# A cross-attention kernel whose whole program stands in another order, with the banks of its scores and the shares of VectorE and GpSimd dealt out anew

## The chip, the cores and the metric

The kernel runs on one core of a Trainium2 chip. A core has five engines, each with an instruction stream of its own that it works off in order: TensorE (PE in the profile; PEld is its weight load), VectorE (DVE), ScalarE (ACT), GpSimd (POOL) and SyncE (SP, which here issues nearly all DMAs). They wait for one another through semaphores. TensorE writes to PSUM, which this kernel uses as eight banks of 128 x 512 float32; the other data lie in SBUF. The metric is the device time of one execution in microseconds, as the median of several runs.

## The reference: cross-attention with two key sets

For two batches of 2048 tokens with 640 channels, and 154 context tokens with 1024 channels (77 of text, 77 of "ip"), the reference computes, in float32:

```python
q = split_heads(x @ Wq.T, 20)                    # 20 heads of 32 channels
k, v = text @ Wk.T, text @ Wv.T                  # 77 keys
k_ip, v_ip = ip @ Wk_ip.T, ip @ Wv_ip.T          # 77 more keys
out = softmax(q k / sqrt(32)) v + softmax(q k_ip / sqrt(32)) v_ip
return out @ Wo.T + bo + x
```

The two softmaxes are separate: each row of 154 scores has two maxima and two sums, of 77 scores each.

## The kernel before, in words

The 20 heads are taken four at a time: a chunk `c` of 128 channels holds four heads of 32 channels, and there are five chunks. A pair (batch `b`, chunk `c`) is a number q = 5b + c from 0 to 9. The 2048 tokens of a batch are two halves of 1024. A unit u = 2q + half, from 0 to 19, is a pair and a half of the tokens; its 1024 tokens are eight tiles of 128 rows, in three blocks s = 0, 1, 2 of three, three and two tiles (`GROUPS`). So there are 60 blocks, 40 wide ones (1848 scores in each partition) and 20 narrow ones (1232).

The order of the program is not left to a planner. One string, `SCHEDULE`, holds 1064 words; the loop at its end emits one word after the other (`emit`), and each engine gets its instructions in the order in which the words that use it stand. So a word's place sets its turn on its own engine, and what it waits for follows from the tiles. The words:

- `q.u.h@n` (L194, TensorE): the queries of unit u for half h of its tokens, in bank n. `cq` (L204, ScalarE) scales them out to SBUF.
- `k.c.t@n`, `v.c.t@n` (L133, TensorE): a projection of keys or values for chunk c, text or ip. `ck` and `cv` (L688, L690, ScalarE) copy them out. `LK.n` loads a weight block for them, `LQ.q` one for queries, `LX.u.h` a block of tokens of the second batch. `SQ.c` (L143, VectorE) transposes the values in squares, `VW` writes them to memory outside the core and `VS` spreads them back.
- For each block s of unit u: `Rs.u@banks` (L226, TensorE) makes the scores of four heads at once, with 32 rows of the array for each head and one bank for each; four digits name the four banks, a single digit 0 or 1 means the lower or upper four. `K` (L238, ScalarE) copies the four banks to SBUF, `M` (L251, VectorE) takes the maxima, `S` (L265) subtracts them, `E` (L272, ScalarE) is the exponential, `D` (L297, VectorE) the sums, `I` (L304, VectorE) their reciprocals, `N` (L309) the normalisation, `T` (L316, VectorE) a transposition in squares of 32. `S` and `N` run on GpSimd, or on VectorE where the word ends in `.d`.
- `A.q@banks` (L325, TensorE): attention times values for both units of pair q, once their six blocks are transposed. `CA.q` (L348, L352, ScalarE) copies the result out.
- First batch's output: `m1` to `m7` (L483, L493) are seven products by half blocks in the manner of Strassen, for each of four groups of tokens, `G` (L424, GpSimd or VectorE) the sums of their token side, `W0` and `W1` (L394, GpSimd) those of the weights, `cm` (L508, L512, VectorE) adds a product to the sum. `o`, `p`, `z` (L464) are the products for the last 128 output channels, `co` and `yz` add them. `fe` fetches the old tokens for a sum, `st` stores a sum.
- Second batch's output, the last part: `F` (L848, TensorE) are 33 products in two halves, `V` (L826, L828) and `X` (L834) their sums of weights and tokens, on VectorE (`.d`) or GpSimd (`.p`), and `Y` (L794, L796, VectorE) adds products to the outputs, which leave as they are done.

Ahead of the schedule stands a fixed beginning: loads, the first queries (in banks 4, 5 and 6) and the first two key projections (banks 2 and 7).

What sets the order around the change is thus the string alone, plus the waits that follow from shared tiles: a bank is written again only once its last reader is done; the scores in SBUF have three zones, so that a unit's copies wait for the attention step that read the zone last; a weight slot is loaded again once its last product is done.

Of the kernel before, what the change touches and what calls it, by code (L numbers as in the profile page):

```python
# [9 lines left out]
F32 = mybir.dt.float32  # L10
# [10 lines left out]
def kernel(  # L21
# [523 lines left out]
    for t in range(2):  # L545
# [227 lines left out]
    for c, stages in enumerate(chains_of):  # L773
        for _, text in stages:
            for _, t in terms(text):
                for h in range(NH):
                    o = int(t[0]), NH * int(t[1]) + h
# [113 lines left out]
```

## Time and profile before

| | us |
|---|---|
| median of 3 runs | 497.94 (497.68 to 498.39) |
| the profiled execution | 498.71 |
| its span, first to last instruction | 496.9 |
| TensorE busy | 490.1 |
| VectorE busy | 441.1 |
| GpSimd busy | 403.7 |
| ScalarE busy | 241.8 |

How to read it: busy time is the union of an engine's instructions as the profile shows them. A matmul's end is modelled and neighbours overlap, so that TensorE can be shown busy while it waits a little. The groups by line give the count, the busy time, the mean length of one instruction in ns, and, behind a bar, the time that the engine was idle just before them with what ended that idle time. In the chain that ended last each row is a start, a length, and the work that the end of the program hung on at that time. `R0.0` and the like in the text are words of the schedule.

The second batch's last part begins behind `A.9` (427 us); ahead of it the scores of both batches, their projections and the first batch's output share TensorE.

### The profile page before, as it was taken

Reading aid. Unit: us, or ns where it says so; the run is one execution under the profiler, and the core shown is the slowest. Engines: PE = TensorE matmul, PEld = TensorE weight load, DVE = VectorE, ACT = ScalarE, POOL = GpSimd, SP = SyncE. Lnnn points to the kernel's source line nnn. Section 1 sums busy time; section 2 is a strip of 40 time slices with the busy share of each in tenths; the row PEclk is TensorE's granted clock in tenths of the full one; section 3 lists DMA queues with packets and bytes.
Section 4 is the critical chain, followed back from the end, with each engine's and each line's share of the span. In section 5 each row is a group of like instructions: output and inputs, shape, how many; then the busy total and the mean of one; then the engine's idle time right before and its main releaser. Section 6 shows DMA issues by size and latency. Waiting matters only on the chain.

```text
span 496.9 us, 9747 instructions
## 1 busy us (share of the span) xinstructions
PE 490.1 (99%) x4114; PEld 288.3 (58%) x4114; DVE 441.1 (89%) x404; ACT 241.8 (49%) x423; POOL 403.7 (81%) x173
## 2 busy tenths in 40 slices
PE   8999999999999999999999999999999999999997
PEld 5658547648647556456655655744766475444442
DVE  0078999999989989998999999799899999999886
ACT  1177557757747568567516635545764443100000
POOL 0079969999989999997995899799599999378770
PEclk9999999999999999999999999999999999999999
DMA  8990543520843835615677079345616012510026
GB/s 258 355 245 12 148 107 84 155 71 22 223 133 80 252 107 162 227 19 154 232 232 247 22 237 319 88 152 176 198 50 175 3 45 64 170 57 29 0 105 233
DMA packets 66988, 70.15 MB, mean 141 GB/s; under 512 B 3712, under 2 KB 46720, under 8 KB 66944
## 3 DMA queue, kind: packets, MB, share of 16 engines
q1 hardware_dynamic: 66224, 68.81, 44.5%
q8 instruction: 32, 0.52, 0.4%
q10 hardware_dynamic: 720, 0.72, 0.4%
q14 instruction: 12, 0.10, 0.1%
HBM read 58.21 MB, written 11.30 MB: 140 GB/s over the span
## 4 chain that ended last, share of the span: by engine, by line
PE 89%; DVE 6%; DMA 3%; SPq 1%; ACT 1%; issue 0%; DVEq 0%
PE bank L194 33%; PE bank L848 11%; PE bank L325 11%; PE bank L226 10%; PE bank L133 9%; PE bank L483 9%; PE bank L464 4%; PE bank L493 2%; DVE pb L316 2%; DMA aT<-in_L_xattn_Wk_ip_dram 2%; DMA wq<-in_L_xattn_Wq_dram 2%; DVE den L297 1%; DVE mx L251 1%; SPq L525 1%; DVE acc L508 0%; DVE acc L512 0%
## 5 line engine op out<-in xcount | busy, mean ns | idle before, releaser
L265 POOL TENSOR_TENSOR pb<-pb,mx 128x1848 f32<-128x1848 f32 (+1 forms) x55 | 162.8, 2980 | 36.0 <-DVE mx L251 35.8
L309 POOL TENSOR_TENSOR pb<-pb,rden 128x1848 f32<-128x1848 f32 (+1 forms) x59 | 172.2, 2940 | 24.0 <-DVE rden L304 21.3
L194 PE MATMUL bank<-x,wq 128*128 128x512 f32 x400 | 179.0, 599 | 0.4 <-DMA wq<-in_L_xattn_Wq_dram 0.2
L251 DVE TENSOR_REDUCE mx<-pb 128x24 f32<-128x1848 f32 (+1 forms) x60 | 109.3, 1841 | 32.2 <-ACT pb L238 32.1
L194 PEld LDWEIGHTS bank<-x,wq 128*128 128x128 f32 x400 | 74.5, 191 | 88.8 <-issue 81.2
L238 ACT COPY pb<-bank 128x462 f32<-128x462 f32 (+1 forms) x240 | 102.0, 537 | 44.5 <-PE bank L226 43.9
L272 ACT ACTIVATE pb<-pb 128x1848 f32<-128x1848 f32 (+1 forms) x60 | 94.2, 1583 | 54.7 <-POOL pb L265 53.9
L297 DVE TENSOR_REDUCE den<-pb 128x24 f32<-128x1848 f32 (+1 forms) x60 | 110.0, 1839 | 5.9 <-ACT pb L272 5.7
L316 DVE STREAM_TRANSPOSE pb<-pb 128x1920 f32<-128x1920 f32 (+1 forms) x60 | 113.9, 1923 | 0.9 <-POOL pb L309 0.8
L226 PEld LDWEIGHTS bank<-kT,qT 32*128 32x128 f32 x1280 | 45.9, 184 | 23.6 <-issue 14.2
L226 PE MATMUL bank<-kT,qT 32*128 32x154 f32 x1280 | 56.5, 305 | 1.0 <-ACT pb L238 0.7
L325 PE MATMUL bank<-pb,v 32*32 32x512 f32 x1600 | 55.2, 597 | 0.1
L204 ACT ACTIVATE qT<-bank 128x512 f32<-128x512 f32 x40 | 23.6, 597 | 52.7 <-PE bank L194 52.7
L133 PE MATMUL bank<-wo_ct,aT 128*128 128x154 f32 x320 | 45.8, 296 | 0.3 <-DMA aT<-in_L_xattn_Wk_ip_dram 0.3
L133 PEld LDWEIGHTS bank<-wo_ct,aT 128*128 128x128 f32 x320 | 43.0, 188 | 4.1 <-issue 2.7
L325 PEld LDWEIGHTS bank<-pb,v 32*32 32x32 f32 x1600 | 29.1, 103 | 23.2 <-issue 11.8
L464 PE MATMUL bank<-aT,wo_ct 128*128 128x512 f32 x80 | 36.3, 596 | 0.0
L483 PE MATMUL bank<-aT,wo_ct 128*128 128x256 f32 x128 | 32.8, 389 | 0.0
L796 DVE TENSOR_TENSOR x<-x,bank 128x512 f32<-128x512 f32 x36 | 23.6, 683 | 5.2 <-PE bank L848 4.6
L483 PEld LDWEIGHTS bank<-aT,wo_ct 128*128 128x128 f32 x128 | 23.3, 190 | 6.4 <-issue 3.7
L464 PEld LDWEIGHTS bank<-aT,wo_ct 128*128 128x128 f32 x80 | 15.0, 190 | 17.3 <-issue 17.1
L848 PE MATMUL bank<-pb 128*128 128x512 f32 x48 | 22.1, 593 | 0.0
(74 smaller groups left out, 348.0 us busy)
## 6 DMA issues: line engine op xcount, KB each, us to landing
x<-in_x_dram SPq DMA_DIRECT2D x20, 1280.0 KB, 6.9
out_dram<-acc SPq DMA_DIRECT2D x20, 256.0 KB, 2.6
x<-in_x_dram SPq DMA_DIRECT2D x18, 256.0 KB, 5.6
acc<-in_x_dram SPq DMA_DIRECT2D x16, 256.0 KB, 4.1
out_dram<-x SPq DMA_DIRECT2D x15, 256.0 KB, 2.0
v<-scr SPq DMA_DIRECT2D x40, 80.0 KB, 4.0
wq<-in_L_xattn_Wq_dram SPq DMA_DIRECT2D x9, 320.0 KB, 5.0
aT<-in_L_xattn_Wk_dram SPq DMA_DIRECT2D x5, 512.0 KB, 7.1
```

The source lines that it names most:

```text
L133: nc.tensor.matmul(keys_in(out), loaded[n][:, k, :], cT[:, k, :, t, :], start=(k == 0), stop=(k == NCC - 1))
L194: nc.tensor.matmul(pq, wqs[q % 3][:, k, :], xs[place_of(u, h)][:, k, :], start=(k == 0), stop=(k == NC - 1),)
L226: nc.tensor.matmul(ps[g][:, ts(t, 2 * L)], qTs[(u, h)][g * D : (g + 1) * D, ts(st, P)], kT[g * D : (g + 1) * D, c, b].rearrange("p t l -> ...
L238: nc.scalar.copy(keys_of(u, s)[:, :, g], ps[g][:, : n * 2 * L].rearrange("p (n l) -> p n l", n=n))
L251: nc.vector.tensor_reduce(mx, rows_of(u, s), AX.X, ALU.max, negate=by_rows(u, s))
L265: eng.tensor_tensor(rows_of(u, s), rows_of(u, s), maxs[(u, s)].unsqueeze(3).to_broadcast([P, n, 2, L]), ALU.subtract)
L272: nc.scalar.activation(e, e, AF.Exp)
L297: nc.vector.tensor_reduce(dens[(u, s)], rows_of(u, s), AX.X, ALU.add)
L309: eng.tensor_tensor(rows_of(u, s), rows_of(u, s), rdens[(u, s)].unsqueeze(3).to_broadcast([P, n, 2, L]), ALU.mult)
L316: nc.vector.transpose(p, p)
L325: nc.tensor.matmul(pa[r][g * D : (g + 1) * D, :], v4s[q % 2][rows, g, k, :], zones[rows, :, g, k, :], start=(k == 0), stop=(k == NK - 1),)
L483: nc.tensor.matmul(part, w_of[m][:, kp, op], t_of(m, b, i)[:, kp], start=(op == kp == 0 and m in (1, 2, 5)), stop=(op == 1 and kp == 1 and ...
```

## The change: the same words in another order

Every word of the one string stands in the other, once, and nothing but the string is changed. What differs:

- the order, from the first word on (before begins with block 2 of unit 0, after with block 0);
- the banks behind `@`, for nearly all score steps and for most queries, projections and products;
- the engine of some sums. Of the subtractions `S`, before has five on VectorE (S1.2, S2.9, S0.10, S2.12, S0.16), after eight (S1.0, S0.2, S1.4, S2.9, S0.10, S0.12, S1.14, S1.15). Of the normalisations `N`, before has N0.12 on VectorE, after N2.7 and N1.16. One `G` sum moves each way, nine `V` and five `X` sums each way;
- `V.P.1` moves ahead of the last transposes, and `LW`, the reload of a part of the output weights, behind the word `A.9`.

The first lines and the lines around `A.9`:

```diff
     SCHEDULE = (
-        "R2.0@2031 K2.0 M2.0 R0.0@6754 K0.0 S2.0 R1.0@1032 K1.0 M0.0 S0.0 q.1.0@7 E2.0 LK.4 M1.0 S1.0 q.1.1@2 "
-        "LK.5 D2.0 I2.0 cq.1.0 R0.1@6157 E0.0 D0.0 I0.0 cq.1.1 R1.1@0243 K0.1 M0.1 N0.0 S0.1 K1.1 k.1.0@6 M1.1 "
...
-        "p.1@4 D1.19 I1.19 D2.19 I2.19 T0.19 m4.3 fe.3.3 cm4.3 st.3.3 p.3@6 N1.19 p.2@7 T1.19 N2.19 T2.19 "
-        "X.B.d@0 A.9@0 V.H.0.d V.P.1.p V.Q.0.d V.T.0.d CA.9 V.T.1.d st.3.1 V.N.0.d X.A.d@1 V.A.0.p V.M.0.d "
...
+        "R0.0@4756 K0.0 M0.0 S0.0 LK.4 R1.0@3012 K1.0 M1.0 q.1.0@4 LK.5 R2.0@1750 K2.0 M2.0 S1.0.d q.1.1@3 "
+        "cq.1.0 LQ.3 S2.0 E0.0 D0.0 I0.0 N0.0 cq.1.1 R0.1@7651 K0.1 R1.1@0423 M0.1 K1.1 M1.1 k.1.0@7 ck.1.0 S0.1 "
...
+        "D1.19 I1.19 fe.3.3 m4.3 cm4.3 V.P.1.d st.3.3 N0.19 T0.19 N2.19 N1.19 T2.19 T1.19 p.1@4 X.L.p@3 p.0@5 "
+        "X.A.d@1 A.9@0132 CA.9 LW V.N.0.d V.G.0.p X.B.d@0 V.U.0.d V.U.1.d V.Q.0.d V.T.0.p V.E.0.d F31.1@0 "
```

Lines of after that hold the places the prediction speaks of (LK.6 and v.1.0; S1.4; N2.7; S1.15; G6.2):

```diff
+        "E1.0 E2.0 k.1.1@6 S1.1 D1.0 R2.1@0457 K2.1 T0.0 E1.1 v.0.0@1 I1.0 N1.0 LK.6 E0.1 M2.1 cv.0.0 D2.0 D1.1 "
+        "I2.0 v.0.1@7 cv.0.1 S2.1 N2.0 q.2.1@4 cq.2.1 v.1.0@5 SQ.0 ck.1.1 D0.1 I1.1 T1.0 cv.1.0 R2.2@4023 K2.2 "
...
+        "N1.3 T1.3 N2.3 q.6.0@3 cq.6.0 S0.4 E0.4 T2.3 S2.4 E2.4 M1.4 S1.4.d D0.4 I0.4 N0.4 A.1@6457 LK.12 E1.4 "
...
+        "E1.7 D2.7 I2.7 N2.7.d R2.8@2013 I0.7 N0.7 cq.9.0 R0.8@4657 D1.7 LK.19 I1.7 K2.8 M2.8 N1.7 K0.8 M0.8 "
...
+        "R2.15@3142 T1.14 m4.1 cq.16.1 E0.15 M1.15 I2.14 K2.15 R2.16@1653 q.17.0@0 fe.1.3 S1.15.d E1.15 K2.16 "
...
+        "K1.17 G6.2 G5.3 S0.17 E0.17 m6.2 cm3.2 LX.18.1 q.18.1@2 st.2.0 fe.3.0 X.I.p@2 M1.17 G4.2 T1.16 "
```

124 rows, old and new, of the table SCHEDULE are left out of this document.

## The prediction

> **What bounds the kernel now.** I read the page's busy times first, then the chain that ended last in order of time, then the busy times in five stretches, then the groups of instructions by shape, the waits, and the timeline at a few places.
>
> ```profile
> PE 490.1 (99%) x4114; PEld 288.3 (58%) x4114; DVE 441.1 (89%) x404; ACT 241.8 (49%) x423; POOL 403.7 (81%) x173
> ```
> ```profile
> 24.04 0.84 PE bank L226 x16
> 25.17 1.07 ACT pb L238 x3
> 26.29 1.07 PE bank L226 x24
> 27.35 8.78 PE bank L194 x20
> 36.13 1.78 PE bank L226 x48
> ...
> 47.48 8.58 PE bank L194 x20
> ...
> 423.53 3.49 DVE pb L316 x2
> 427.06 5.13 PE bank L325 x138
> 432.22 0.66 ACT aT L352 x2
> ...
> 445.20 48.15 PE bank L848 x112
> 493.37 0.69 DVE x L796
> ```
> The chain is TensorE nearly throughout. It leaves it at 25.17 (score copies), before the last attention step at 427.06 (transposes), at 432.22 (copies of that step) and for the last sum at 493.37. The stretches say how full TensorE is; the columns are the stretch, its length, then busy time and instructions of PE, PEld, DVE, ACT and POOL, and the granted clock, which is 1.00 all along:
>
> ```profile
> 28.00:107.00 79.00, 78.98 (x675) 49.34 (x690) 74.46 (x55) 50.68 (x87) 72.26 (x25) 1.00 0.43 115
> 107.00:212.00 105.00, 104.89 (x1136) 63.69 (x1115) 99.67 (x78) 70.48 (x129) 100.35 (x36) 1.00 0.49 144
> 212.00:304.00 92.00, 92.00 (x792) 55.13 (x779) 87.02 (x72) 47.87 (x83) 79.39 (x33) 1.00 0.53 174
> 304.00:427.00 123.00, 122.96 (x1095) 75.02 (x1094) 117.30 (x107) 63.60 (x102) 111.56 (x49) 1.00 0.37 119
> 427.00:497.00 70.00, 65.93 (x300) 29.15 (x300) 61.03 (x95) 2.31 (x8) 39.12 (x27) 1.00 0.26 94
> ```
> From 28 to 427 TensorE idles 0.02 + 0.11 + 0 + 0.04 = 0.17 us. VectorE idles 4.5 + 5.3 + 5.0 + 5.7 = 20.5 us there. So TensorE is the bound, and VectorE stands close behind it with some 5% of room. A new order can win only what TensorE still waits, and can lose as much as it makes TensorE wait.
>
> **The change, part by part.** TensorE's list holds the same 231 steps of the order in both kernels, so its work is the same except where kinds of work meet. Two query steps between other full-array work take 8.58 us (47.48), the two behind a score step 8.78 (27.35): leaving row-tiled work (scores, attention) costs about 0.2. The order of before has 49 such stretches of row-tiled work, that of after 50: +0.2, or +0.3 if entering costs a little too. I take **+0.3**.
>
> The start. Before begins with R2.0, R0.0, R1.0, and R1.0 takes the banks of R2.0, so it waits until these are copied: R2.0 starts at 24.04, R1.0 at 26.29, and the timeline shows TensorE idle for 0.66 us just before it:
>
> ```profile
> 26.29 1.07 PE L226 MATMUL bank<-kT,qT 32*128 32x154 f32 x24 [0.66 <-ACT pb L238]
> L238 ACT COPY pb<-bank 128x462 f32<-128x462 f32 x160 | 76.1, 586 | 30.4 <-PE bank L226 30.4
> 14.34 8.65 SPq L166 DMA_DIRECT2D x<-in_x_dram  x10
> x<-in_x_dram SPq DMA_DIRECT2D x18, 256.0 KB, 5.6
> aT<-in_L_xattn_Wv_dram SPq DMA_DIRECT2D x5, 512.0 KB, 5.3
> ```
> After begins with R0.0 in banks 4, 7, 5, 6 and R1.0 in 3, 0, 1, 2, all different, so this wait goes: **-0.7**. What is late next is q.1.0 in bank 4. It would start at 24.04 + two wide score steps (1.78 in the row at 36.13) + 0.1 = 25.9; the first copy of bank 4 starts about 1.1 after R0.0 (25.17 is 1.13 after 24.04) and takes 0.6, so it ends at 25.8. Its x slices are the first five of the ten issued from 14.34 to 22.99; the fifth leaves at about 18.1, plus 5.6 to landing gives 23.7. If they came 2 us later the gain would be gone and a loss of 1.3 stand there; I count -0.7.
>
> VectorE and GpSimd. These rows set the prices:
>
> ```profile
> L265 POOL TENSOR_TENSOR pb<-pb,mx 128x1848 f32<-128x1848 f32 x37 | 122.9, 3332 | 8.8 <-DVE mx L251 8.7
> L316 DVE STREAM_TRANSPOSE pb<-pb 128x1920 f32<-128x1920 f32 x40 | 85.5, 2146 | 0.2 <-POOL pb L309 0.2
> L251 DVE TENSOR_REDUCE mx<-pb 128x24 f32<-128x1848 f32 x40 | 81.9, 2058 | 5.1 <-ACT pb L238 5.0
> L272 ACT ACTIVATE pb<-pb 128x1848 f32<-128x1848 f32 x40 | 70.0, 1757 | 44.8 <-POOL pb L265 44.0 <-DVE pb L265 0.7
> L309 DVE TENSOR_TENSOR pb<-pb,rden 128x1848 f32<-128x1848 f32 x1 | 2.1, 2085 | 0.0
> L304 DVE RECIPROCAL rden<-den 128x24 f32<-128x24 f32 x40 | 11.6, 295 | 1.1
> ```
> Wide subtractions on VectorE go from 3 to 7, narrow ones from 2 to 1, narrow normalisations from 0 to 1 (wide ones stay at 1). That is +4 x 2.09 = **8.3 us more on VectorE** (the narrow two cancel) and 4 x 3.33 = **13.3 us less on GpSimd**. The G, V and X sums of the two engines are exchanged one for one (3, 19 and 11 on VectorE in both). VectorE's 20.5 us of idle would shrink to 12.2. On TensorE this costs nothing as long as the transposes ahead of each attention step A.n end in time, so I set the two lists against each other at the places where that is tightest. An instruction of VectorE starts about 0.07 before the one ahead is shown to end (two transposes, wide and narrow, take 3.49 in the chain), so prices are the means less 0.07.
>
> At A.3, before: behind the last scores R1.8 TensorE has R1.8, a query step and a projection, 7.6 us, and A.3 follows. VectorE needs the scores (1.0), their four copies (2.0 with the 0.586 of each, overlapped), the maximum M1.8 (1.99) and the transpose T1.7 (2.08): 7.1. Room 0.5, and no idle shows on TensorE there. In after, exactly this group stands ahead of A.3 and also, as R1.6, M1.6, T1.5, ahead of A.2: room 0.5 at both. At A.4, before has 21.1 us of TensorE from R1.9 against 20.4 of VectorE, after 21.7 from R2.9 against 20.9: 0.7 and 0.8. At A.0, A.1 and A.5 to A.9 the same count leaves 0.8 to 1.9 in after (1.0 to 2.3 in before). So the rooms are smaller by a few tenths but of a size that held before; I add **+0.1 to +0.3** for them.
>
> Why should VectorE's idle shrink rather than its end come later? Part of it is a wait for a result that the order asks for too soon:
>
> ```profile
> 35.32 2.08 DVE L297 TENSOR_REDUCE den<-pb 128x24 f32<-128x1848 f32 x1 [1.56 <-ACT pb L272]
> 148.11 2.08 DVE L297 TENSOR_REDUCE den<-pb 128x24 f32<-128x1848 f32 x1 [1.41 <-ACT pb L272]
> 118.64 1.51 DVE L316 STREAM_TRANSPOSE pb<-pb 128x1280 f32<-128x1280 f32 x1 [0.49 <-POOL pb L309]
> DVE mx L251 <- ACT pb L238: 32.1, 10, 25.3
> ```
> Between a maximum and the sum of the same block GpSimd subtracts (3.33) and ScalarE takes the exponential (1.76): 5.2 with hand-overs that other work on VectorE must cover. In before that cover falls short by 1.7 at S0.0 and 1.5 at S1.6, the two waits of 1.56 and 1.41; over all 60 blocks, with the normalisations, by 4.7. In after it falls short once, by 0.3. And where VectorE waits for scores (32.1 less the first 25.3 is 6.8 us), a VectorE that is later waits less. 4.4 and 6.8 together exceed 8.3.
>
> The copies and transfers. Each bank of a score step is freed by its own copy; walked in the same way, the tightest of after are within 0.3 us of those of before. One new tight place is G6.2 on GpSimd ahead of m6.2, with 0.2 us: **+0.1**, up to 0.5. On SP the tightest transfer is the weight block LK.6, free to leave when v.0.0 is done at about 44.9; v.1.0 needs it at 51.3, and 5.3 to landing leaves 1.1 us. Behind A.9 the first products reuse the banks of A.9 in both kernels, so the 0.66 at 432.22 stays, and the weights and sums of the last part stand at least 4 us ahead of their products in both.
>
> Two engines on one memory. VectorE's subtraction reads two tensors:
>
> ```profile
> 215.12 2.42 DVE L265 TENSOR_TENSOR pb<-pb,mx 128x1848 f32<-128x1848 f32 x1
> 215.56 3.12 POOL L394 TENSOR_TENSOR x<-wo_ct,x 128x512 f32<-128x512 f32 x1
> 263.37 2.55 DVE L265 TENSOR_TENSOR pb<-pb,mx 128x1232 f32<-128x1232 f32 x1
> 264.56 2.50 POOL L424 TENSOR_TENSOR x<-aT 128x512 f32<-128x512 f32 x1
> 196.00 1.43 DVE L265 TENSOR_TENSOR pb<-pb,mx 128x1232 f32<-128x1232 f32 x1
> ```
> The narrow one took 1.43 at 196.00 and 2.55 at 263.37, with GpSimd at work; the wide one 2.42 against 2.09 alone. GpSimd's own then took 3.12 and 2.50. So over the six such operations of before VectorE lost 0.3 + 1.1, some 0.25 each; the four net new ones cost 1.0 at that rate. In after most stand where GpSimd has nothing to do by the lists (S1.4 and N2.7 before the tight places A.2 and A.3 do). I count nothing for them on TensorE, as VectorE's idle covers 1 us; the worst case is a rival below.
>
> [...]
>
> **The sum.** +0.3 (one more stretch) - 0.7 (the start) + 0.2 (rooms) + 0.1 (m6.2) = -0.1 us, on a profiled execution of 498.71 (span 496.9 and 1.8 around it). That execution is 0.8 above the median of the runs, 497.94, so I forecast 497.8 for the runs. Within 0.2%, 1.0 us, is about what a measurement can't tell from no change.
>
> **The rivals.**
> *VectorE becomes the bound* (slower). Place: A.2 to A.4. From 107 to 212 VectorE idled 5.3 us; S1.4 and N2.7 add 3.4 there. If its waits do not shrink, TensorE stalls by 3.4 less the room of 0.5, +2.9: 500.7; if half of them do, +1.2: 499.1. It decides from the point where VectorE still idles over 2.4 us in that stretch. For it: VectorE and GpSimd are both 95% busy there. Against it: the same groups of steps held at A.3.
> [...] If the four new operations meet GpSimd as the one at 263.37 did, VectorE loses 4 x 1.1 and GpSimd as much; with G6.2 and N1.16 in one place m6.2 would start 1 to 2 us late: 499.4.
> *TensorE loses its last waits* (faster). 0.7 at the start, 0.17 later, and short waits hidden under the modelled ends of matmuls that the idle time does not show, about as much again as the start: -1.5 + 0.3 = -1.2, 496.7. Against it: the rooms are no larger than before.
>
> **How the numbers follow.** No change 0.50; VectorE 0.20; the port 0.12; faster 0.18. The likeliest's own range is 496.9 to 498.9. The range reaches down to the faster case, 496.6, and up to most of VectorE's, 500.4.
>
> **What would show it.** Right: R1.0 starts without idle at about 25; TensorE's idle from 28 to 427 stays under 1 us; VectorE's busy time is some 8 us up, GpSimd's 13 down; VectorE's two long waits for the exponential are gone. Wrong: idle on TensorE ahead of attention steps put down to VectorE's transposes, at A.2 to A.4 first; VectorE's idle from 107 to 212 above 2.4; GpSimd instructions stretched by over 1 us beside the new subtractions; q.1.0 waiting for x.

## The result and the profile after

The changed kernel takes 502.57 us (median of 6 runs, 501.74 to 504.07), against 498.16 (497.50 to 499.06) for the kernel before in the same comparison. The ratio is 1.0091, with a 95% interval of 1.0071 to 1.0111: it is 4.4 us slower. The prediction of 497.8 was wrong, and the time lies above its range (496.6 to 500.4). The profiled execution of after took 502.97, its span 501.2.

First the busy times of the profile after, and its five stretches (the columns are those of the prediction; the last stretch is longer because the program is):

```profile
PE 491.5 (98%) x4114; PEld 288.5 (58%) x4114; DVE 449.2 (90%) x408; ACT 242.1 (48%) x423; POOL 392.8 (78%) x169
```
```profile
28.00:107.00 79.00, 78.98 (x705) 49.61 (x704) 76.36 (x57) 50.14 (x90) 69.96 (x24) 1.00 0.44 115
107.00:212.00 105.00, 104.76 (x1137) 63.72 (x1128) 103.77 (x80) 71.49 (x129) 96.11 (x35) 1.00 0.51 151
212.00:304.00 92.00, 92.00 (x807) 55.06 (x792) 86.59 (x74) 49.17 (x83) 80.28 (x32) 1.00 0.53 170
304.00:427.00 123.00, 122.38 (x1094) 74.52 (x1062) 117.90 (x103) 62.11 (x101) 108.01 (x45) 1.00 0.37 116
427.00:501.00 74.00, 67.52 (x300) 30.18 (x300) 63.27 (x97) 2.31 (x8) 37.59 (x29) 0.98 0.25 89
```

From 28 to 427 TensorE idles 0.02 + 0.24 + 0 + 0.62 = 0.88 us, 0.7 more than before; 0.26 of it, behind 426.7, already belongs to the wait ahead of A.9. The long middle, where 60 blocks of scores go through VectorE and GpSimd and where the prediction looked hardest, cost next to nothing. The last stretch is different: 6.5 us idle where before had 4.1, and a granted clock of 0.98 where every stretch of before had 1.00. The chain of waits of after, cut to its beginning and to the place where TensorE leaves it:

```profile
23.81 1.97 PE bank L226 x46
25.78 4.49 PE bank L194 x10
...
420.79 3.35 DVE pb L828
424.13 0.62 DVE pb L316
424.76 1.39 issue
426.15 3.53 DVE pb L316 x2
429.68 0.04 issue
429.73 6.73 PE bank L325 x145
```

At the start the score steps follow one another without a break, so the start gains as forecast. At the end a piece of 3.35 us stands in the chain that the prediction never priced: `V.P.1` (L828), a sum of two 128 x 128 blocks of the output weights on VectorE. The timeline of after there, GpSimd's row, then VectorE's two, then TensorE's two:

```profile
415.24 8.74 POOL L309 TENSOR_TENSOR pb<-pb,rden 128x1848 f32<-128x1848 f32 x3
420.70 3.43 DVE L828 TENSOR_TENSOR pb<-pb,wo_ct 128x128 f32<-128x128 f32 x1
424.06 5.62 DVE L316 STREAM_TRANSPOSE pb<-pb 128x1920 f32<-128x1920 f32 x3
429.73 7.12 PE L325 MATMUL bank<-pb,v 32*32 32x512 f32 x160 [2.99 <-DVE pb L316]
437.18 1.98 PE L848 MATMUL bank<-x,wo_ct 128*128 128x512 f32 x4 [0.33 <-ACT aT L352]
```

`V.P.1` took 3.43 us. Other sums of the same shape take 0.29 where nothing stands beside them. It ended at 424.13, just behind GpSimd's run of three normalisations (N0.19, N2.19, N1.19), which ends at 423.98. The last three transposes stand behind it on VectorE and wait; A.9, the last attention step, needs them and starts after 2.99 us of idle. Then A.9 itself takes 7.12 us, where its 160 products take 5.52 in the runs below. The stretches of 2 us around it say why; the granted clock is the third number from the end:

```profile
428.00:430.00 2.00, 0.27 (x16) 0.24 (x32) 2.00 (x2) 0.00 (x0) 0.00 (x0) 1.00 1.00 343
430.00:432.00 2.00, 2.00 (x65) 0.77 (x34) 2.00 (x3) 0.00 (x0) 0.00 (x0) 0.78 0.60 229
432.00:434.00 2.00, 2.00 (x52) 1.24 (x35) 1.19 (x6) 0.00 (x0) 0.87 (x2) 0.50 0.00 0
434.00:436.00 2.00, 2.00 (x69) 1.65 (x61) 0.41 (x2) 0.00 (x0) 0.46 (x1) 0.87 0.03 8
```

The clock falls to 0.50 shortly behind the idle. The three rows with 0.78, 0.50 and 0.87 over 2 us each come to 0.44 + 1.00 + 0.26 = 1.7 us of clock lost, or about 3.4 us at 0.50. Four of the six executions have a mean clock of 0.997, which is the size of one such fall (0.003 of 501 us is 1.5); the two longest (503.50 and 504.07) have 0.993, about twice the loss. So the loss reads off two rows: 2.99 of idle and 7.12 - 5.52 = 1.6 of half clock, 4.6 together, against the 4.4 measured. That was the theory to be tested: **one small sum, in the way of GpSimd, holds up the transposes, and the clock adds half as much again.** The rivals: VectorE, with 8 us more work, is late in general and `V.P.1` only the last straw (*load*); what makes `V.P.1` long is not GpSimd but something it waits for in its queue (*queue wait*); and the clock fell for another reason than the idle. The expectations call the theory of the sum *port* and the queue wait *operand*; the runs show that the sum waits and until when, and no port.

### The profile page after: what moved, and what is told of

It is laid out like the page before. It is cut to its first block, busy times and chain, and to the rows that moved or that the text cites. A ratio compares the mean times of both kernels' runs of the same rounds, so it can differ in the third digit from the quotient of the medians.

```text
span 501.2 us, 9755 instructions
## 1 busy us (share of the span) xinstructions
PE 491.5 (98%) x4114; PEld 288.5 (58%) x4114; DVE 449.2 (90%) x408; ACT 242.1 (48%) x423; POOL 392.8 (78%) x169
## 4 chain that ended last, share of the span: by engine, by line
PE 92%; DMA 3%; DVE 2%; SPq 1%; issue 1%; ACT 0%
PE bank L194 33%; PE bank L848 11%; PE bank L325 11%; PE bank L483 10%; PE bank L226 10%; PE bank L133 8%; PE bank L464 6%; PE bank L493 3%; DMA aT<-in_L_xattn_Wk_ip_dram 2%; DMA wq<-in_L_xattn_Wq_dram 2%; DVE pb L316 1%; SPq L525 1%; DVE pb L828 1%; ACT pb L238 0%; DVE acc L508 0%
## 5 line engine op out<-in xcount | busy, mean ns | idle before, releaser
L265 POOL TENSOR_TENSOR pb<-pb,mx 128x1848 f32<-128x1848 f32 (+1 forms) x52 | 153.3, 2966 | 34.0 <-DVE mx L251 33.8
L325 PE MATMUL bank<-pb,v 32*32 32x512 f32 x1600 | 56.9, 614 | 3.2 <-DVE pb L316 3.0
L325 PEld LDWEIGHTS bank<-pb,v 32*32 32x32 f32 x1600 | 31.1, 104 | 26.8 <-issue 11.6
```

The source lines that it names most:

```text
L265: eng.tensor_tensor(rows_of(u, s), rows_of(u, s), maxs[(u, s)].unsqueeze(3).to_broadcast([P, n, 2, L]), ALU.subtract)
L325: nc.tensor.matmul(pa[r][g * D : (g + 1) * D, :], v4s[q % 2][rows, g, k, :], zones[rows, :, g, k, :], start=(k == 0), stop=(k == NK - 1),)
```

## The experiments

### The sum on GpSimd, at the same place

```diff
- ... cm4.3 V.P.1.d st.3.3 N0.19 T0.19 N2.19 ...
+ ... cm4.3 V.P.1.p st.3.3 N0.19 T0.19 N2.19 ...
```


> The kernel after with one word changed: the small sum V.P.1 (128 x 128) runs on GpSimd instead of VectorE, in the same place of the order. Theory 'port': in after V.P.1 took 3.43 us instead of 0.29, because GpSimd had just begun the normalisation N1.19 and both engines read two tensors; the last three transposes came 3.1 late, TensorE idled 2.99 ahead of A.9, and A.9 took 7.12 instead of 5.52 at a granted clock of 0.50. Then everything goes at once: A.9 starts at 426.7 or so, takes 5.5, and the median is 502.6 - 3.0 - 1.6 = 498.0 or up to 0.5 less (497.5 to 498.2). Rival 'load': VectorE has 8.3 us more work and is late at A.9 for that reason; then taking 0.3 us off its list saves 0.3 us, perhaps 0.5, and the median stays at 502.

Measured: 498.10 (497.72 to 499.01, 11 runs), ratio to before 1.0000, interval 0.9991 to 1.0009. The timeline of this kernel at the same place:

```profile
415.38 8.75 POOL L309 TENSOR_TENSOR pb<-pb,rden 128x1848 f32<-128x1848 f32 x3
420.42 3.56 DVE L316 STREAM_TRANSPOSE pb<-pb 128x1920 f32<-128x1920 f32 x2
426.39 5.52 PE L325 MATMUL bank<-pb,v 32*32 32x512 f32 x160
```

A.9 starts 3.3 us earlier, with no idle ahead of it, and takes 5.52. One letter in a string of 1064 words takes back all 4.4 us. VectorE's other additional work is still there, so *load* is out.

### The sum on VectorE, behind the last transposes

```diff
- ... cm4.3 V.P.1.d st.3.3 N0.19 T0.19 N2.19 N1.19 T2.19 T1.19 p.1@4 ...
+ ... cm4.3 st.3.3 N0.19 T0.19 N2.19 N1.19 T2.19 T1.19 V.P.1.d p.1@4 ...
```


> The kernel after with V.P.1 still on VectorE, but moved behind the last transpose T1.19, so that VectorE's list is as long as in after. Port: A.9 no longer waits for it, 497.5 to 498.2, as with V.P.1 on GpSimd. Load: the transposes end 0.3 us earlier, the median stays at about 502.

Measured: 497.98 (497.39 to 498.51, 10 runs), ratio 0.9994, interval 0.9984 to 1.0003. The timeline of this kernel on VectorE and TensorE:

```profile
420.88 5.62 DVE L316 STREAM_TRANSPOSE pb<-pb 128x1920 f32<-128x1920 f32 x3
426.43 0.61 DVE L828 TENSOR_TENSOR pb<-pb,wo_ct 128x128 f32<-128x128 f32 x1
426.85 5.52 PE L325 MATMUL bank<-pb,v 32*32 32x512 f32 x160
```

The engine, the operation and the work are those of after; the transposes start at 420.88, while GpSimd is in the midst of its run (from 415.42, 8.73 long), and are not held up. The sum takes 0.61 here, and nothing on TensorE waits for it.

### TensorE kept busy while A.9 waits

```diff
             at[name] = banks_at(where)
+            if x == 9:
+                for _ in range(3):
+                    nc.tensor.matmul(
+                        at[name][0], wo[:, 0, ts(NC - 1, P)], rows_of_attention(1, 0)[:, 0], start=True, stop=True
+                    )
             attend(x, at[name])
```
Three products of 128 x 512 go into a bank that A.9 overwrites; `V.P.1` stays where after has it.

> The kernel after with three more products (128 x 512, 0.86 us each, 2.6 us in all) ahead of A.9 on TensorE, into a bank that A.9 then overwrites; their results are not used. They fill most of TensorE's idle time of 2.99 us and leave the start of A.9 where it is, at 429.7. Theory 'clock': A.9 is slow only because TensorE stood idle before it; then the granted clock stays at 1.00, A.9 takes 5.5 us, and the median falls by 1.6, to 501.0. Rival: A.9's 7.12 us come from something else (its operands, the transposes); then the median stays at 502.6.

Measured: 501.12 (500.93 to 501.67), ratio 1.0060, interval 1.0046 to 1.0074. A.9 in this kernel's timeline:

```profile
429.56 5.52 PE L325 MATMUL bank<-pb,v 32*32 32x512 f32 x160 [0.41 <-DVE pb L316]
```

A.9 starts as late as in after (429.56 against 429.73), but takes 5.52 and not 7.12, and 1.45 us of the time come back. So the slow A.9 came from the idle ahead of it, and not from its data or from anything beside it.

### One such product instead of three

```diff
-                for _ in range(3):
+                for _ in range(1):
```


> One product of 128x512 (some 0.4 us) is added just ahead of A.9's first stretch on TensorE; it writes a bank that A.9 overwrites, so the output stays the same. It tells how long an idle drops the granted clock. In after the idle before A.9 was 2.99 us and the clock fell to .50 in 432 to 434; with three products 0.41 us and A.9 took 5.52 us. The idle here should be about 2.1 to 2.6 us. If an idle of that length is enough, A.9 takes about 7.1 us and the time is 502.3 to 502.9, as in after. If it is not, A.9 takes 5.5 us and the time is 500.7 to 501.4. V.P.1 itself should still take about 3.4 us either way.

Measured: 502.8, one run. This kernel's timeline, and its stretch from 432 to 434:

```profile
429.56 7.12 PE L325 MATMUL bank<-pb,v 32*32 32x512 f32 x160 [2.13 <-DVE pb L316]
```
```profile
432.00:434.00 2.00, 2.00 (x49) 1.28 (x34) 1.14 (x5) 0.00 (x0) 0.87 (x2) 0.50 0.04 8
```

The product took 0.86 us of the idle (2.99 less 2.13), and not some 0.4. In this execution 2.13 us of idle was enough for the clock to fall, and the price is the same 1.6 us as after 2.99, while 0.41 us cost nothing. That such an idle does not always bring the fall is shown by the runs of the next experiment.

### The same edit in before

```diff
- ... D2.19 I2.19 T0.19 m4.3 ... A.9@0 V.H.0.d V.P.1.p V.Q.0.d ...
+ ... D2.19 I2.19 V.P.1.d T0.19 m4.3 ... A.9@0 V.H.0.d V.Q.0.d ...
```


> The kernel before with V.P.1 moved from GpSimd to VectorE, ahead of the last three transposes (behind I2.19), and nothing else. There VectorE would reach it at 420.7, while GpSimd normalises without a break from 416.5 to 425.2 (8.73 us for three). Theory 'port, one instruction': V.P.1 waits until the running normalisation ends at 423.0, the transposes and A.9 come 2.6 later, and the median rises by 2.6 and by what the idle TensorE costs in clock, to 500.8 to 502.4. Theory 'port, whole run': it waits until GpSimd has nothing queued, at 425.2; +4.9 and the clock, 503 to 505. Rival 'load': 0.3 us more on VectorE's list, 498.5.

Measured: 501.32 (500.65 to 502.37) against 498.22, ratio 1.0062, interval 1.0046 to 1.0077. The timeline of this kernel, and a stretch of it:

```profile
415.45 8.79 POOL L309 TENSOR_TENSOR pb<-pb,rden 128x1848 f32<-128x1848 f32 x3
419.59 2.53 DVE L828 TENSOR_TENSOR pb<-pb,wo_ct 128x128 f32<-128x128 f32 x1
428.50 7.12 PE L325 MATMUL bank<-pb,v 32*32 32x512 f32 x160 [2.62 <-DVE pb L316]
```
```profile
430.00:432.00 2.00, 2.00 (x49) 0.93 (x33) 1.97 (x5) 0.00 (x0) 0.00 (x0) 0.50 0.99 345
```

In another order, with the old shares of VectorE and GpSimd, the one moved word makes the same picture: a wait for GpSimd, idle, half clock. Here `V.P.1` came in the midst of GpSimd's second instruction of three and ended at 422.1, 2.1 us ahead of the end of the run: it did not wait for the third.

The four executions fall into two pairs. Two have a mean clock of 0.997 (501.77, the profiled one, and 502.37). In the other two it is 1.000, and they take 500.87 and 500.65, some 2.5 us above before, near the idle alone. So by the times the wait comes in each, but the clock falls only in two. That A.9 is slow only with an idle ahead of it stands for these runs; that the idle always brings it does not.

### The sum ahead, but earlier

```diff
- ... cm7.3 D2.19 I2.19 p.2@7 D1.19 I1.19 fe.3.3 m4.3 cm4.3 V.P.1.d st.3.3 ...
+ ... cm7.3 D2.19 I2.19 V.P.1.d p.2@7 D1.19 I1.19 fe.3.3 m4.3 cm4.3 st.3.3 ...
```


> The kernel after with V.P.1 moved ahead of D1.19 and I1.19 (behind I2.19), still on VectorE. VectorE reaches it at 416.9, inside GpSimd's N0.19 (415.2 to 418.5), with N2.19 queued behind it until 420.7; N1.19 cannot be queued, as I1.19 stands behind V.P.1. One instruction: it starts at 418.5, D1.19 and N1.19 come 1.9 later, the last transpose ends at 427.8 or so, A.9 starts 1.8 earlier than in after: median 499.2 to 500.8, by the clock. Whole run: it starts at 420.7, the last transpose ends at 429.6 to 430.3, the median is 502.5 to 503.5, as in after or worse. Load: 502.6, as in after.

Measured: 498.80 (498.49 to 498.95), ratio 1.0008, interval 0.9994 to 1.0023, so less was lost than expected, and no loss is clear of the noise. The timeline of this kernel on GpSimd, VectorE and TensorE:

```profile
415.06 5.54 POOL L309 TENSOR_TENSOR pb<-pb,rden 128x1848 f32<-128x1848 f32 x2
416.65 1.84 DVE L828 TENSOR_TENSOR pb<-pb,wo_ct 128x128 f32<-128x128 f32 x1
427.10 5.52 PE L325 MATMUL bank<-pb,v 32*32 32x512 f32 x160 [0.54 <-DVE pb L316]
```

The sum arrives while N0.19 runs (one alone takes 3.29 us) and waits for its end: it takes 1.84 us and ends at 418.49. The normalisation queued behind N0.19 starts at 418.30 and does not hold it longer. In after it arrived at 420.70, just as the third normalisation began (the run ends at 423.98, and a wide one takes 3.29), and so it waited for the whole of that one. So "one instruction" is what the runs show, and the sum waited for what was left of that instruction at its arrival: 3.14 us in after, nearly all of it, and 1.55 here, half (3.43 and 1.84, less the 0.29 of the sum alone). What would decide a tie, had the sum come a little sooner, no run shows.

### Another operation in the place of the sum

The third question is what in `V.P.1` waits. Two kernels put another instruction on the same tile and place; both leave out the subtraction of block 34 of the weights.

```diff
+            if (w, j) == ("P", 1):
+                eng.tensor_scalar(out, out, -1.0, None, ALU.mult)
```


> The kernel after with V.P.1 in its place on VectorE, but as an operation with one tensor as input (the sum is multiplied by -1 in place); the subtraction of the block 34 of the output weights is left out. [...] Rival 'operand': V.P.1 waited for its data or for its place in the queue, whatever it computes; then it takes 3.4 us here too and the run takes 502 to 503.

Measured: 502.63, one run. The timeline of the kernel with one operand:

```profile
420.36 3.36 DVE L824 TENSOR_SCALAR pb<-pb 128x128 f32<-128x128 f32 x1
429.31 7.11 PE L325 MATMUL bank<-pb,v 32*32 32x512 f32 x160 [2.92 <-DVE pb L316]
```

I had expected no wait here, and a time of about 498. The expectation failed: this instruction, which reads one tensor, took 3.36 us where the sum took 3.43, so reading two was not needed for the wait. It does not read the weights either, so these are not what the sum waited for. It left open whether the wait is for GpSimd at all, so the next kernel put a transposition in squares there, an operation that VectorE runs 60 times in this kernel (the two at 420.42 in the first experiment took 3.56 us together, inside GpSimd's run):

```diff
+            if (w, j) == ("P", 1):
+                eng.transpose(out, out)
```


> The kernel after with V.P.1 in its place on VectorE, but as a transposition in squares of 32 of the same tile in place; the subtraction of the block 34 of the output weights is left out. The operation with one input (the multiplication by -1) still took 3.36 us there. The wide transposes of this kernel ran beside GpSimd at 2.08 to 2.18 us, so they do not contend. Port: the transposition takes 0.3 us in the same place, with the same tile to wait for, A.9 starts at about 426.7 and one run takes about 498. Operand: it waits for the tile or its turn, 3.4 us, and the run takes 502 to 503.

Measured: 497.99, one run. The timeline of the kernel with the transposition:

```profile
420.39 0.30 DVE L824 STREAM_TRANSPOSE pb<-pb 128x128 f32<-128x128 f32 x1
426.35 5.52 PE L325 MATMUL bank<-pb,v 32*32 32x512 f32 x160
```

The same tile, the same place, the same moment, 0.30 us: so it was no wait for the tile or for a place in the queue. Which operation stood there decided whether it waited: the sum took 3.43 us (0.29 alone), the multiplication 3.36, the transposition 0.30. Both kernels ran once. They show the wait, and not what it comes from.

### Eight other steps of VectorE back on GpSimd

```diff
- S1.0.d  S0.2.d  S1.4.d  S0.12.d  S1.14.d  S1.15.d  N2.7.d  N1.16.d  V.P.1.d
+ S1.0    S0.2    S1.4    S0.12    S1.14    S1.15    N2.7    N1.16    V.P.1.p
```
This is the order and the banks of after without VectorE's larger share of the subtractions and normalisations. It goes further than before's share: VectorE keeps two of these steps, S2.9 and S0.10, where before has six.

> The kernel after with V.P.1 on GpSimd, and also the six subtractions (S1.0, S0.2, S1.4, S0.12, S1.14, S1.15) and two normalisations (N2.7, N1.16) back on GpSimd that after has on VectorE and before has not. VectorE gets 15.9 us less, GpSimd 25 more. Theory: VectorE's extra share fills idle time and costs TensorE nothing, but in this order GpSimd has to have it: back on GpSimd each costs 1.2 us more than on VectorE in the chain of its block, where the room is 0.5 to 1.9 us; the median is 498 to 501. Rival 'load': VectorE's share is what costs time in after; then this is faster than the 498.0 of V.P.1 on GpSimd alone, by up to 1.

Measured: 511.02 (509.34 to 512.5), ratio 1.0253, interval 1.0224 to 1.0283: the largest miss among the expectations. I had thought of the shares as nearly free in either direction. The timeline of this kernel from 264 to 276, on GpSimd, ScalarE, VectorE and TensorE:

```profile
264.06 6.53 POOL L265 TENSOR_TENSOR pb<-pb,mx 128x1848 f32<-128x1848 f32 x2 [3.65 <-DVE mx L251]
270.62 3.38 ACT L272 ACTIVATE pb<-pb 128x1848 f32<-128x1848 f32 x2 [9.64 <-POOL pb L265]
273.90 2.27 ACT L352 COPY aT<-bank 128x256 f32<-128x256 f32 x8
274.10 2.08 DVE L297 TENSOR_REDUCE den<-pb 128x24 f32<-128x1848 f32 x1 [7.71 <-ACT pb L272]
274.58 1.13 PE L226 MATMUL bank<-kT,qT 32*128 32x154 f32 x4 [2.20 <-ACT aT L352]
```

S1.12 and S0.12 now stand one behind the other on GpSimd. The two exponentials wait for them, the copies of A.5 stand behind the exponentials in ScalarE's queue, and R0.13 needs the banks that these copies free. TensorE idles 2.20 us there, and again the clock falls behind it, to 0.50 from 276 to 282. Of the four executions two have a mean clock of 0.990 (512.50, the profiled one, and 512.39) and two of 0.996 and 0.997 (509.65, 509.34).

### One of the eight on VectorE again

```diff
- ... N2.10 T2.10 M0.12 S0.12 S1.12 m4.0 ...
+ ... N2.10 T2.10 M0.12 S0.12.d S1.12 m4.0 ...
```


> The run with eight subtractions and normalisations back on GpSimd (511.02), with one of them, S0.12, given to VectorE again. There TensorE lost 6.8 us between 268 and 283 (2.27 ahead of R0.13, 2.49 ahead of m2.1, 2.07 ahead of R1.13). If the cause is the one read from its trace (S1.12 and S0.12 one behind the other on GpSimd, the exponentials late, the copies of A.5 behind these in ScalarE's queue, the banks of R0.13 late), these three losses go and the time is 503.5 to 505.5. If S0.12 is not what holds A.5's copies, R0.13 still waits over 1 us and the time stays above 508.

Measured: 504.73, one run, inside the 503.5 to 505.5 of the reading. The timeline of this kernel on ScalarE and TensorE, and, last, one step of TensorE later in this kernel and the same step in the kernel of 511.02:

```profile
266.95 1.75 ACT L272 ACTIVATE pb<-pb 128x1848 f32<-128x1848 f32 x1 [0.74 <-DVE pb L265]
268.60 2.28 ACT L352 COPY aT<-bank 128x256 f32<-128x256 f32 x8
273.07 1.07 PE L226 MATMUL bank<-kT,qT 32*128 32x154 f32 x24
```
```profile
367.74 2.00 PE L483 MATMUL bank<-aT,x 128*128 128x256 f32 x8 [1.78 <-POOL aT L424]
373.79 3.17 PE L483 MATMUL bank<-aT,x 128*128 128x256 f32 x8 [1.78 <-POOL aT L424]
```

The copies of A.5 start 5.3 us earlier, R0.13 starts without idle, and the clock stays full. One subtraction on the other engine was worth some 6 us here, from 4.6 to 7.8 by the execution of the kernel of 511.02 that it is compared with. Part of that is the clock and not the subtraction: ahead of the step in the last two lines TensorE idles 1.78 us in both kernels, and the clock stays at 1.00 behind it here but falls to 0.61 and 0.53 (374 to 376 and 376 to 378) there, so that the step takes 3.17 and not 2.00. The other seven stand for the rest between 498.10 and 504.73; they were not taken one by one.

### A version that might beat both

The version with `V.P.1` behind the transposes still loses a little, by the lengths of the steps, ahead of the first query step of unit 8 (0.30 us). One more edit gives that step another bank:

```diff
- ... I1.5 q.8.0@1 VW.6 ...
+ ... I1.5 q.8.0@4 VW.6 ...
```


> After with V.P.1 behind the last transpose (as in the run in which it stands there, 497.98) and one more edit: the q step of block 8 given a later place, because after lost 0.30 us there. If both steps were rightly named, the time is 497.5 to 498.0 and the ratio to before 0.9985 to 0.9996; if the 0.30 us only moves to the next step, it is 497.9 to 498.3 and the ratio 0.9990 to 1.0003. A time above 499 would mean that the later place delays something that needs block 8's q, and the idle would stand ahead of that step on TensorE.

Measured: 497.91 (497.70 to 498.77, 11 runs), against 497.90 (14 runs), ratio 1.0001, interval 0.9992 to 1.0011. (The step kept its place in the order; only its bank changed, to one that is free earlier, and not "a later place" as the expectation says.) The loss there went from 0.30 to 0.12, and the wait ahead of A.4 grew from 0.13 to 0.26: most of it moved on. No version here is measurably faster than before.

## Why the prediction was wrong

**The step that failed** is in "VectorE and GpSimd": "The G, V and X sums of the two engines are exchanged one for one (3, 19 and 11 on VectorE in both)", with no price. Counted by engine that is true. But one of the words exchanged, `V.P.1.p` behind A.9, became `V.P.1.d` ahead of the last transposes, where the queue had almost no room, and beside a run of GpSimd that was 8.7 us long. The working had what it needed to price it: the move itself, which the description of the change names, and the rows that showed a narrow subtraction on VectorE at 2.55 instead of 1.43 beside GpSimd. It read those as a rate, 0.25 us for each such operation. One more row of before shows that they held a wait:

```profile
258.07 6.55 POOL L265 TENSOR_TENSOR pb<-pb,mx 128x1848 f32<-128x1848 f32 x2
```

GpSimd's last instruction there ended at 264.62 (258.07 + 6.55); 1.43 us more is 266.05, and the subtraction ended at 265.92. So it waited for the rest of that instruction and then ran at its own length. The wait depended on where the operation landed (none at 196.00, 1.12 us at 263.37), and an average over six says little about one. The working set its rate only against the four new subtractions and normalisations, and `V.P.1` had no term; it took 3.43.

**The room at A.9 was set too large.** "At A.0, A.1 and A.5 to A.9 the same count leaves 0.8 to 1.9 in after": at A.9 the room was about 0.2. With the transposition of 0.30 us in its place the last transposes end at 426.2 and A.9 starts at 426.35, right behind the product before it. The wait of 3.14 more than alone, less that room, is the idle of 2.99.

**A term for the clock was absent.** No term and no rival had a clock that falls behind an idle; every row of before had 1.00, and I took that for granted. It is 1.6 of the 4.4 us. With the term for the sum at 3.0 and this at 1.6, the forecast of 497.8 would have been 502.4, against 502.57 measured.

**The rivals.** *The port* (0.12, the rival with 499.4) came nearest, at another place than I gave it. That two engines share a port was not shown: the runs show the wait and where it ends. I looked for the new subtractions and normalisations beside m6.2, and let a 128 x 128 sum pass as too small to matter. The sum of 0.29 us waited 3.14, and the narrow subtraction of 1.43 at 263.37 waited 1.12: each for what was left of GpSimd's instruction, and neither by its own length. The price of 499.4 was also too low, as it scaled the wait from that one subtraction and had no clock in it. *VectorE becomes the bound* at A.2 to A.4 did not happen: its stated point was 2.4 us of idle from 107 to 212, and it had 105.00 - 103.77 = 1.23, but TensorE idled 0.24 there and not 1.2 or 2.9. *TensorE loses its last waits* did not happen either; the interval of the best version holds 1.0000.

**What held.** The first score steps follow one another (23.81, 1.97 long, then the query step at 25.78), so the wait of 0.66 at the start went. With `V.P.1` out of the way the change comes to 498.10 and 497.98, within 0.3 us of the 497.8 forecast: the rest of the sum, -0.1, agrees with ratios of 1.0000 and 0.9994. Its single terms were not measured apart, and each of these intervals is about 0.9 us wide, more than any term, so that part of this may be luck. VectorE's busy time rose by 8.1 us, which is near 8.3 only by chance, since 3.1 of it is `V.P.1` waiting. GpSimd's fell by 10.9, not 13.3. The groups of after for the wide subtractions, and two of GpSimd's rows from its timeline, show a part of why:

```profile
L265 DVE TENSOR_TENSOR pb<-pb,mx 128x1848 f32<-128x1848 f32 x7 | 14.8, 2121 | 0.2
L265 POOL TENSOR_TENSOR pb<-pb,mx 128x1848 f32<-128x1848 f32 x33 | 109.4, 3322 | 31.5 <-DVE mx L251 31.3
```
```profile
33.94 4.02 POOL L265 TENSOR_TENSOR pb<-pb,mx 128x1232 f32<-128x1232 f32 x1 [1.68 <-DVE mx L251]
195.99 4.42 POOL L265 TENSOR_TENSOR pb<-pb,mx 128x1848 f32<-128x1848 f32 x1 [0.49 <-DVE mx L251]
```

VectorE's wide subtractions hardly waited (2.12 on average against 2.09). GpSimd's did: a narrow one took 4.02 us (2.26 on average in before) beside VectorE's new S1.0, and a wide one 4.42 (3.32 on average) beside S2.9, which stands on VectorE in both kernels. The prediction had named GpSimd instructions stretched by over 1 us as a sign of being wrong; they came, fell on GpSimd, and cost TensorE next to nothing (0.02 us of idle from 28 to 107, 0.24 from 107 to 212). VectorE's idle from 28 to 427 went from 20.5 to 14.4, not to 12.2, and TensorE's is 0.88 us, inside the "under 1 us" of the prediction.

One thing about the middle I had not seen: the shares are no small correction to the order. With eight of VectorE's ten subtractions and normalisations back on GpSimd, the same order costs 511 us. What it costs with exactly before's share, no run shows.

## What to carry to other kernels

Price a moved instruction by what runs beside it at its new place, not by its own length: here a sum of 0.29 us on VectorE took 3.43 beside GpSimd's work and held up all that stood behind it, and a place a few words later made it free (497.98 against 502.57). Go through the queue ahead of each step that the bound engine waits for, and look at the small words too. Where the bound engine is TensorE, look at the clock behind an idle too: here an idle of 2.13 to 2.99 us ahead of A.9 cost 1.6 us on top of its length, though not in every execution.

## What the runs showed of the hardware that was not expected

- Beside one of GpSimd's normalisations, VectorE's `tensor_scalar` with one float32 tensor of 128 x 128, in and out in SBUF, waited as long (3.36 us) as a subtraction with two (3.43); a transposition in squares on the same tile didn't wait (0.30).
- The wait lasted until the end of the GpSimd instruction that ran at the arrival, and not of those queued behind it: the sum took 1.84 and 2.53 us in all when it came in the midst of one, 3.43 when it came as one began.
- TensorE's clock fell to 0.50 after an idle of 2.13, 2.20, 2.62 and 2.99 us in the profiled executions, and not after 0.41, 0.54, 0.95 or 1.17 (the last two in the kernel of 504.73). The length alone did not decide: after 1.78 us it fell in one kernel and not in another, and of four executions of before with the sum ahead, two had a mean clock of 0.997 and two of 1.000. What else decides, no run shows. In the rows of after the loss comes to about 3.4 us at 0.50, from 430 to 436.
